# Moving the power of the degrees, and the turn of its result, from the head of the dilation into its turns

## The chip, the cores and the metric

The kernel runs on one core of one Trainium2 chip. The metric is the device time of one execution in microseconds (us). Before the change three timed executions took 2714.34, 2714.92 and 2715.22 us; their median, 2714.92 us, is the time before.

The engines are named as the profile names them: PE multiplies matrices (PEld loads its weights), DVE and ACT are the vector and the scalar engine, POOL is GpSimd, and SP issues most of the transfers. Each engine works through its own list of instructions in order and waits at an instruction until what it needs is there.

## The reference

Four layers of a graph network run one after the other on 16 batches of 1024 nodes with 128 features and one adjacency matrix per batch. Each layer adds its result to `x` and normalises the rows.

- Layer 0 is an attention over the neighbours with a gate.
- Layer 1 first dilates the adjacency matrix: row by row it removes some neighbours of a node, in the row and in the column, so that a row depends on the rows before it. Three graph convolutions with the dilated matrix follow.
- Layer 2 is a second gated attention with the original matrix.
- Layer 3 is a graph convolution with the original matrix, scaled on both sides by the inverse root of the degrees:

```python
def _gcn_norm(adj):
    A_hat = adj + jnp.eye(adj.shape[-1], dtype=adj.dtype)
    deg = A_hat.sum(axis=-1)
    dinv = jnp.where(deg > 0, jax.lax.rsqrt(deg), 0.0)
    return dinv[..., :, None] * A_hat * dinv[..., None, :]
```

`dinv` is what the changed lines compute. The degrees are summed in layer 0, while the matrices are read; nothing reads `dinv` before layer 3.

## The kernel before

**Stages.** In the profiled execution layer 0 runs to about 624 us, the dilation to about 1000 us, layer 1 to about 1670 us, and layers 2 and 3, interleaved batch by batch, to the end. A last piece computes a flag from several checks of the data, `nomem` among them.

**Degrees.** `deg` is a tile of 128 partitions by 128 columns (16 batches of 8 blocks). ACT fills it by the accumulator of the copy that turns the matrix into 8 bits (L931). `dinv` is another name for the same tile (L673), and `zeros` another name for `mx0` (L681), the row extrema of layer 0's attention. `mhalf` holds -0.5.

**The head of the dilation** (L1178 to L1188), in the order of the source: DVE compares `mx0` and reduces it to `nomem`; DVE writes `zeros` from `deg`, and the shifted degree into `deg`; POOL takes the power -1/2 in place (L1183); PE transposes the result into a PSUM tile `pt` that shares its two buffers with the tile `s` of the removals (L1185); DVE copies it into `dt` (L1187); SP stores `dt` into `dinv_d` in device memory (L1188). In layer 3 every batch reads `dinv_d` as a row (L1754) and `dinv` as columns (L1758).

**The dilation.** The rows are taken in 8 blocks of 128 and the batches in 2 groups of 8, which makes 16 steps. `prepare` counts a step's neighbours (products L1069 over four batches at a time; L1063, L1071 and L1072 on DVE). `fixed_point` finds the removals inside the block by iteration (L1092, L1097 and L1104 on DVE, products L1100). `removal` applies them for one batch: products L1144 and L1142 into `s`, ACT L1145, DVE L1148 and L1149, products L1152 to L1156, ACT L1157. A turn `i` interleaves the fixed point of step `i`, the removals of step `i - 1` and the preparation of the step after next. There are 16 turns.

**The end of layer 0** runs together with the first preparations and the first fixed point: `after` of the last batch, which ends in `normed`. Its row norm takes a power on POOL too (L745, 128 by 8 values, called from L797), between L742 on DVE before it and L799 on DVE behind it; then ACT scales the rows (L801, eight instructions) and POOL stores the result (L1019).

**What sets the order.** The source gives each instruction a place, but the framework's scheduler lists the instructions of each engine by its own model of when they are ready, with the place in the source as priority. An instruction can so stand on its engine far ahead of its place in the source. The kernel takes powers on POOL alone; POOL's list around this place is: power of the degrees, L745 of the last batch, L1019, and then nothing until the stores of the dilated matrices (L1159). SP's list is: the store L1188, layer 1's weights (L703, L693, L698), the loads of the dilated matrices (L1369).

Of the kernel before, what the change touches and what calls it, by code (L numbers as in the profile page):

```python
# [9 lines left out]
F32 = mybir.dt.float32  # L10
# [7 lines left out]
OP = mybir.AluOpType  # L18
AX = mybir.AxisListType
# [3 lines left out]
P = 128  # L23
# [616 lines left out]
def fast_kernel(ctx: ExitStack, tc: tile.TileContext, t: dict, out: bass.AP, flag: bass.AP):  # L640

    nc = tc.nc
    B, N, D = t["x"].shape
    NT = N // P
    H2 = N // 512
    BT = B * NT
# [4 lines left out]
    identf = consts.tile([P, P], F32, name="identf")  # L651
# [5 lines left out]
    mhalf = consts.tile([P, NT], F32, name="mhalf")  # L657
# [10 lines left out]
    dinv_d = dram.tile([BT, P], F32, name="dinv_d")  # L668
# [3 lines left out]
    deg = consts.tile([P, BT], F32, name="deg")  # L672
    dinv = deg  # L673
# [6 lines left out]
    mx0 = consts.tile([P, BT], F32, name="mx0")  # L680
    zeros = mx0  # L681
    nodeg = consts.tile([P, B], F32, name="nodeg")
    nc.vector.memset(nodeg, 1.0)
    nomem = consts.tile([P, 1], F32, name="nomem")
# [126 lines left out]
    def take_turns(streams):  # L811
        while streams:
            streams = [s for s in streams if next(s, streams) is not streams]
# [221 lines left out]
    with ExitStack() as ph:  # L1035
        sb = ph.enter_context(tc.tile_pool(name="dl_sb", bufs=2, side="right", reuse_waits="tile"))
# [3 lines left out]
        ps_s = ph.enter_context(tc.tile_pool(name="dl_ps", bufs=2, space=PSUM, side="right", reuse_waits="tile"))  # L1040
# [120 lines left out]
        def removals(now, then):  # L1161

            start = prepare(*then) if then else None
            for i in range(GB):
                removal(*now, i)
                yield
                if then and i % QB == QB - 1:
                    next(start)
                    yield
# [5 lines left out]
        ending.close()  # L1175
        ps_c = ph.enter_context(tc.tile_pool(name="dl_pc", bufs=2, space=PSUM, reuse_waits="tile"))

        nc.vector.tensor_scalar(mx0, mx0, 1.0e15, None, op0=OP.is_gt)  # L1178
        nc.vector.tensor_reduce(nomem, mx0, AX.X, OP.max)

        nc.vector.tensor_scalar(zeros, deg, -1.0, float(N), op0=OP.mult, op1=OP.add)
        nc.vector.tensor_scalar(deg, deg, 1.0, 1.0, op0=OP.add, op1=OP.max)
        nc.gpsimd.tensor_tensor(dinv, deg, mhalf[:, 0:1].to_broadcast([P, BT]), op=OP.pow)  # L1183
        pt = ps_s.tile([BT, P], F32, name="pt", tag="s")
        nc.tensor.transpose(pt, dinv, identf)  # L1185
        dt = sb.tile([BT, P], F32, name="dt", bufs=1)
        nc.vector.tensor_copy(dt, pt)  # L1187
        nc.sync.dma_start(dinv_d, dt)  # L1188

        for i in range(1, len(steps) + 1):  # L1190
            streams = [fixed_point(*steps[i])] if i < len(steps) else []
            streams.append(removals(steps[i - 1], steps[i - 1 + G2] if i - 1 + G2 < len(steps) else None))
            take_turns(streams)

    class Layers23:

# [640 lines left out]
def kernel(tc: tile.TileContext, t: dict, out: bass.AP):  # L1837
    nc = tc.nc
    with tc.tile_pool(name="flag", bufs=1) as pool:
        flag = pool.tile([1, 1], I32, name="flag")  # L1840
        fast_kernel(tc, t, out, flag)
        with tc.If(nc.values_load(flag[0:1, 0:1]) != 0):
            general_kernel(tc, t, out)
# [22 lines left out]
```

## Time and profile before

| What | Value |
|---|---|
| median of the timed executions | 2714.92 us |
| the profiled execution, its own time | 2712.03 us |
| span from its first to its last instruction | 2710.2 us |
| PE busy | 2540.1 us (94%) |
| DVE busy | 2085.2 us (77%) |
| ACT busy | 1977.6 us (73%) |
| POOL busy | 317.9 us (12%) |
| PE clock, mean of what was granted | 0.98 of full speed |
| POOL, power of the degrees (L1183), 128 by 128 values | 1 instruction, 20.74 us |
| POOL, power L745 of a norm, 128 by 8 values, typical | 1.66 us |
| SP, `dinv_d` stored | issued at 645.97 us |
| SP, `dinv_d` first read (L1754) | issued at 1673.3 us |

The profile is one execution with a record for each instruction. Shares of busy time are averages over stages that differ, so the prediction reads the stage around the change by itself: busy time by stage, who waited for whom, and the list of instructions in order of time. A wait that the profile shows is put down to the instruction that came last.

### The profile page before, as it was taken

How to read it: one execution, taken by the hardware profiler on the slowest of the kernel's cores; microseconds unless marked ns; L12 is line 12 of the kernel's file. 1: busy time of each engine (PE TensorE's matmuls, PEld its weight loads, DVE VectorE, ACT ScalarE, POOL GpSimd, SP SyncE). 2: the span in 40 equal slices, each digit the busy share in tenths (PEclk: the TensorE clock that was granted, in tenths of full speed). 3: DMA queues.
4: the chain of work that ended last, by engine and by line, in shares of the span. 5: the costliest groups of instructions: out<-in, count | busy, mean ns of one | idle time of the engine just before them, and what ended most of it. 6: DMA issues, size and time to landing. Idle time of an engine off the chain costs nothing.

```text
span 2710.2 us, 41446 instructions
## 1 busy us (share of the span) xinstructions
PE 2540.1 (94%) x14888; PEld 1677.4 (62%) x14888; DVE 2085.2 (77%) x5590; ACT 1977.6 (73%) x3188; POOL 317.9 (12%) x287
## 2 busy tenths in 40 slices
PE   8999999996889879999999998999999999999986
PEld 4445444443666647887788886466666666666655
DVE  6887778875799876776688876577877878787785
ACT  7888889874888866666655544777777777777773
POOL 0000000003000001111212133000110100001001
PEclk9999999996999989999999999999999999999998
DMA  5555555430000052233466664102212111111100
GB/s 190 161 174 171 172 163 179 156 117 23 2 2 2 2 207 75 95 106 128 139 227 212 250 231 181 39 24 70 78 70 85 71 63 63 63 63 63 47 24 25
DMA packets 120808, 285.34 MB, mean 105 GB/s; under 512 B 12305, under 2 KB 65425, under 8 KB 113425
## 3 DMA queue, kind: packets, MB, share of 16 engines
q1 hardware_dynamic: 101280, 203.33, 23.1%
q0 software_dynamic: 19312, 79.28, 7.6%
q8 instruction: 119, 1.95, 0.3%
q14 instruction: 97, 0.79, 0.1%
HBM read 202.72 MB, written 79.82 MB: 104 GB/s over the span
## 4 chain that ended last, share of the span: by engine, by line
PE 56%; DVE 16%; issue 7%; POOL 5%; ACT 4%; DMA 3%; POOLq 0%; ACTq 0%; DVEq 0%
PE ph L1618 8%; PE acc L1678 7%; PE acc L1306 6%; PE ph L766 5%; PE acc L973 5%; PE pmm L724 5%; PE ph L759 4%; PE ph L1432 3%; PE pmm L1690 3%; PE ph L1605 2%; DVE mid L1097 2%; DVE keep L1148 2%; POOL rn L745 2%; POOL ln_rstd L745 1%; ACT q L1145 1%
## 5 line engine op out<-in xcount | busy, mean ns | idle before, releaser
L745 POOL TENSOR_TENSOR ln_rstd<-ln_rstd,mhalf 128x8 f32<-128x8 f32 (+1 forms) x68 | 108.4, 1594 | 1332.0 <-DVE ln_rstd L742 861.4
L973 PE MATMUL acc<-em,hs 128*128 128x512 f32 x512 | 259.2, 607 | 2.5 <-DVE past L1075 1.3
L724 PE MATMUL pmm<-xT,G 128*128 128x512 f32 x512 | 259.8, 604 | 0.0
L1678 PE MATMUL acc<-ex,hs 128*128 128x512 f32 x512 | 248.9, 596 | 7.5 <-DVE hs L1705 4.5
L801 ACT ACTIVATE xn<-xn,ln_nb,ln_rstd 128x128 f32<-128x128 f32 x512 | 204.6, 481 | 55.3 <-DVE ln_nb L799 55.3
L1306 PE MATMUL acc<-a,hi 128*128 128x512 f32 x768 | 233.7, 398 | 12.0 <-DVE a L1293 9.0
L1306 PE MATMUL acc<-a,lo 128*128 128x512 f32 x768 | 230.1, 394 | 5.8 <-DVE lo L1273 5.8
L985 ACT ACTIVATE em<-em,mx 128x1024 f32<-128x1024 f32 x128 | 146.3, 1143 | 53.0 <-DVE mx L983 51.5
L983 DVE CUSTOM_DVE_ANT_0 em<-pmm,msk 128x1024 f32<-128x1024 f32 x128 | 156.1, 1220 | 31.9 <-PE pmm L724 30.7
L1698 ACT ACTIVATE ex<-em,mn 128x1024 f32<-128x1024 f32 x128 | 146.9, 1147 | 44.7 <-DVE mn L1695 44.0
L1690 PE MATMUL pmm<-G,hT 128*128 128x512 f32 (+3 forms) x416 | 175.3, 523 | 0.1
L1695 DVE CUSTOM_DVE_ANT_0 em<-pmm,msk 128x1024 f32<-128x1024 f32 x128 | 155.4, 1214 | 24.4 <-PE pmm L1692 22.3
L1306 PEld LDWEIGHTS acc<-a,hi 128*128 128x128 f32 x768 | 142.2, 189 | 43.5 <-DVE a L1293 11.5
L1306 PEld LDWEIGHTS acc<-a,lo 128*128 128x128 f32 x768 | 143.3, 189 | 41.1 <-DVE lo L1273 11.5
L1157 ACT ACTIVATE carry<-pc,negone 128x1024 fp8e4<-128x1024 f32 x128 | 141.3, 1115 | 27.6 <-PE pc L1156 24.8
L931 ACT ACTIVATE carry<-an 128x1024 fp8e4<-128x1024 f32 x128 | 134.4, 1050 | 31.3 <-DMA an<-in_adj 30.4
L980 ACT ACTIVATE msk<-carry,l0nbig 128x1024 bf16<-128x1024 fp8e4 x128 | 145.3, 1136 | 0.0
L1686 ACT ACTIVATE msk<-A,nbig 128x1024 bf16<-128x1024 fp8e4 x128 | 144.2, 1138 | 0.0
L1618 PE MATMUL ph<-A,hi 128*128 128x512 f32 x512 | 143.1, 420 | 0.8 <-DVE zn L1607 0.6
L1295 ACT CAST a<-A 128x1024 fp32r<-128x1024 fp8e4 x96 | 98.4, 1048 | 54.9 <-PE acc L1306 53.8
L1678 PEld LDWEIGHTS acc<-ex,hs 128*128 128x128 f32 x512 | 88.6, 190 | 76.8 <-issue 54.6
L1295 ACT CAST a<-carry 128x1024 fp32r<-128x1024 fp8e4 x96 | 99.1, 1047 | 47.8 <-PE acc L1306 47.5
(319 smaller groups left out, 6184.2 us busy)
## 6 DMA issues: line engine op xcount, KB each, us to landing
an<-in_adj SPq DMA_DIRECT2D x128, 512.0 KB, 3.7
adj_d<-carry POOLq DMA_DIRECT2D x16, 1024.0 KB, 4.2
A<-dil_d SPq DMA_DIRECT2D x16, 1024.0 KB, 5.3
rdeg<-rdeg_d SPq DMA_DIRECT2D x32, 512.0 KB, 4.1
A<-adj_d SPq DMA_DIRECT2D x16, 1024.0 KB, 5.0
ag_d<-ag POOLq DMA_DIRECT2D x24, 512.0 KB, 5.0
ag<-ag_d SPq DMA_DIRECT2D x24, 512.0 KB, 6.1
xn<-in_x SPq DMA_DIRECT2D x16, 512.0 KB, 4.3
```

The lines of the kernel that those rows point to most:

```text
L724: nc.tensor.matmul(p[:, h * 512:(h + 1) * 512], lhsT, rhs[:, h * 512:(h + 1) * 512], start=True, stop=True)
L745: nc.gpsimd.tensor_tensor(r, r, mhalf[:, :n], op=OP.pow)
L801: nc.scalar.activation(r[:, k.start + i, :], r[:, k.start + i, :], AF.Identity, scale=rstd[:, i:i + 1], bias=nb[:, i:i + 1])
L973: nc.tensor.matmul(s.acc[:, c], hs, em[:, c], start=(jt == 0), stop=(jt == NT - 1))
L983: nc.vector.tensor_tensor_reduce(em, e, msk, 1.0, 3.0e38, op0=OP.add, op1=OP.min, accum_out=mn)
L1295: nc.scalar.copy(a, A[:, 2 * i:2 * i + 2, c])
L1306: nc.tensor.matmul(acc, part[:, jt, :], pieces[h * NT // 2 + k][:, jt - 2 * k, :], start=(part is parts[0] and jt == 0), stop=(part is par ...
L1618: nc.tensor.matmul(p, part[:, jt, :], A[jt][:, c], start=(jt == 0 and i == 0), stop=(jt == NT - 1 and i == 1))
L1678: nc.tensor.matmul(s.acc[:, c], hs, ex[:, c], start=(jt == 0), stop=(jt == NT - 1))
L1690: nc.tensor.matmul(e[:, c], s.hT[:, js], s.G[:, c], start=True, stop=True)
L1695: nc.vector.tensor_tensor_reduce(row, e, msk, 1.0, 0.0, op0=OP.add, op1=OP.min, accum_out=mn)
L1698: nc.scalar.activation(ex, row, AF.Exp, scale=-1.0, bias=mn, accum_out=sm)
```

## The change

The eleven lines at the head of the dilation go into the loop over its turns. The DVE operations and the power are issued after the streams of turn 2, the transpose, its copy and the store after those of turn 6. The operations themselves are the same, and so are the tiles and the pools.

```diff
-        nc.vector.tensor_scalar(mx0, mx0, 1.0e15, None, op0=OP.is_gt)
-        nc.vector.tensor_reduce(nomem, mx0, AX.X, OP.max)
-
-        nc.vector.tensor_scalar(zeros, deg, -1.0, float(N), op0=OP.mult, op1=OP.add)
-        nc.vector.tensor_scalar(deg, deg, 1.0, 1.0, op0=OP.add, op1=OP.max)
-        nc.gpsimd.tensor_tensor(dinv, deg, mhalf[:, 0:1].to_broadcast([P, BT]), op=OP.pow)
-        pt = ps_s.tile([BT, P], F32, name="pt", tag="s")
-        nc.tensor.transpose(pt, dinv, identf)
-        dt = sb.tile([BT, P], F32, name="dt", bufs=1)
-        nc.vector.tensor_copy(dt, pt)
-        nc.sync.dma_start(dinv_d, dt)
-
         for i in range(1, len(steps) + 1):
             streams = [fixed_point(*steps[i])] if i < len(steps) else []
             streams.append(removals(steps[i - 1], steps[i - 1 + G2] if i - 1 + G2 < len(steps) else None))
             take_turns(streams)
+            if i == 2:
+                nc.vector.tensor_scalar(mx0, mx0, 1.0e15, None, op0=OP.is_gt)
+                nc.vector.tensor_reduce(nomem, mx0, AX.X, OP.max)
+
+                nc.vector.tensor_scalar(zeros, deg, -1.0, float(N), op0=OP.mult, op1=OP.add)
+                nc.vector.tensor_scalar(deg, deg, 1.0, 1.0, op0=OP.add, op1=OP.max)
+                nc.gpsimd.tensor_tensor(dinv, deg, mhalf[:, 0:1].to_broadcast([P, BT]), op=OP.pow)
+            elif i == 6:
+                pt = ps_s.tile([BT, P], F32, name="pt", tag="s")
+                nc.tensor.transpose(pt, dinv, identf)
+                dt = sb.tile([BT, P], F32, name="dt", bufs=1)
+                nc.vector.tensor_copy(dt, pt)
+                nc.sync.dma_start(dinv_d, dt)
```

## The prediction

> **What bounds the kernel now.** I began with the busy table: PE is busy 94% of 2710.2 us, so time can be won only where PE stands still. The forty slices show one such hole: PE at 6 of ten in the tenth slice, the only slice where POOL shows 3. The chain that ended last confirms it: POOL holds 5% of it, and in the stretch around the hole one POOL instruction is on it for 20.75 us. Busy time by stage, cut at the instruction's own ends (columns: stage, length, busy us and count for PE, PEld, DVE, ACT, POOL, then PE clock, DMA share, GB/s):
>
> ```profile
> 610.00:624.40 14.40, 12.60 (x59) 5.74 (x58) 8.50 (x35) 9.36 (x18) 2.65 (x3) 1.00 0.13 38
> 624.40:645.10 20.70, 1.61 (x34) 1.07 (x32) 1.17 (x5) 1.02 (x1) 20.68 (x1) 0.62 0.00 0
> 645.10:662.10 17.00, 13.53 (x125) 8.66 (x126) 13.65 (x58) 4.00 (x7) 1.80 (x1) 0.50 0.05 13
> 662.10:1000.00 337.90, 286.46 (x3710) 210.31 (x3709) 292.03 (x831) 274.70 (x366) 5.23 (x9) 0.95 0.08 29
> ```
>
> For 20.7 us everything but POOL is idle, and afterwards PE runs at half clock. Who waits for whom there (us in total, times, longest):
>
> ```profile
> ACT r L777 <- PE pq L775: 20.5, 1, 20.5
> ...
> PE pt L1185 <- POOL deg L1183: 19.1, 1, 19.1
> DVE dt L1187 <- PE pt L1185: 18.4, 1, 18.4
> POOL ln_rstd L745 <- DVE thr L1092: 15.2, 1, 15.2
> ...
> DVE ln_nb L799 <- POOL ln_rstd L745: 1.5, 1, 1.5
> ```
>
> The transpose L1185 waits for the power; the gate products L775 stand behind it on PE and ACT waits for them; on DVE the copy L1187 holds up the rest. The timeline (start, duration, instruction, idle before it):
>
> ```profile
> 624.35 20.74 POOL L1183 TENSOR_TENSOR deg<-deg,mhalf 128x128 f32<-128x128 f32 x1 [5.87 <-DVE deg L1182]
> ...
> 626.78 0.29 DVE L1063 TENSOR_TENSOR uY<-carry,upper 128x128 int32<-128x128 int32 x1
> ...
> 645.14 0.48 PE L1185 MATMUL pt<-identf,deg 128*128 128x128 f32 x1 [19.13 <-POOL deg L1183]
> ...
> 645.54 1.08 PE L775 MATMUL pq<-hpT,l0gw 128*32 128x256 f32 x8
> 645.65 0.29 DVE L1187 COPY dt<-pt 128x128 f32<-128x128 f32 x1 [18.43 <-PE pt L1185]
> ...
> 660.24 1.80 POOL L745 TENSOR_TENSOR ln_rstd<-ln_rstd,mhalf 128x8 f32<-128x8 f32 x1 [15.16 <-DVE thr L1092]
> ...
> 662.08 0.17 DVE L799 SCALAR_TENSOR_TENSOR ln_nb<-ln_mv,ln_rstd 128x8 f32<-128x8 f32 x1 [1.53 <-POOL ln_rstd L745]
> ```
>
> The next POOL instruction, the power of the last batch's norm (L745), comes 15.16 us after the long one ended. Those 15 us, not the 20, will turn out to be the prize.
>
> [...]Where DVE was first, POOL lost time:
>
> ```profile
> 1772.11 1.21 DVE L1752 TENSOR_TENSOR A<-A,identb 128x1024 fp8e4<-128x1024 fp8e4 x1
> 1772.37 2.45 POOL L745 TENSOR_TENSOR ln_rstd<-ln_rstd,mhalf 128x8 f32<-128x8 f32 x1 [22.67 <-ACT msk L1686]
> ```
>
> That is 2.45 us against the usual 1.64 to 1.66. But L1063 above reads two SBUF tiles, starts 2.43 us into the long power and takes 0.29 us, as it does outside it (0.28 at 649.59). The power does not shut DVE out for its length; the measurement decides. [...]Here PE stops at 626.02 and the clock mean of 0.79 for 629 to 630 puts the drop at about 629.6, that is 3.6 us.
>
> **The change, part by part.** Source order and built order differ: the framework lists each engine's instructions by readiness in its own model. Comparing the two built programs, the four DVE operations and the power do not move at all. On DVE they still stand between an L1063 and an L1071 of the opening preparation, and on POOL the power is still directly ahead of the last L745. What moves is the tail: the transpose goes on PE to just ahead of the last L1100 group but one of turn 6, the copy on DVE to behind L1117 a little later, the store on SP from ahead of the layer 1 weight loads to behind them, still ahead of the first dil_d load. Around the new place a few L1142, L1144, L1148, L1063 and L1071 swap neighbours; the rest is unchanged apart from semaphore names.
>
> *Removed at the head.* PE's 19.1 us wait, DVE's 18.4 us, and 0.48 + 0.29 us of work. L775 can follow the end of hpT (625.14 + 1.02 = 626.16) at about 626.25 instead of 645.54: 19.3 us earlier. DVE's L1089 follows L1087 at 627.2 instead of 645.86: 18.7 us earlier. From there to L742 the chain is nearly all DVE work, so L742 moves from 659.94 to about 641.
>
> *What is late next.* POOL is in order and still busy until 624.35 + 20.74 = 645.09. So L745 starts there, 4 us after its input (L742's, though the waits name L1092) is ready, and takes 1.65: it ends at about 646.8 instead of 662.04. L799 on DVE and the eight L801 on ACT wait for it, and behind them in order everything of DVE and ACT, then PE at L1100. From L799 on the two kernels have the same order, so the head gains 662.04 − 646.8 = 15.2 us, not 19.3. The chain of waits should show a DVE wait on L745 of 5.5 to 6 us in place of 1.5.
>
> *The power under traffic.* Before, it ran beside an idle DVE; now DVE works beside it. The DVE operations with two SBUF inputs between L1089 and L742, with L1148 counted in, are L1097 (2 × 1.23), L1013 and L1016 (1.22 each), L1113 (2 × 0.29), L1063 (0.28), L1148 (0.74), L1149 (0.42) and ten small ones (about 0.12 each in a row): 8.1 us. If each stopped POOL's reading[...], the power would last 8 us longer; that is the upper bound. The lower is 0. A power of 8 columns takes 1.64 and one of 128 takes 20.74, so 0.16 us a column; a 1.65 us power that starts 0.02 us ahead of a 0.69 us cast (1121.52) loses nothing, [...]1.22 us is the work of 7.7 columns. I take 0.7 us.
>
> *The clock.* PE was at half clock from 645.1 to 662.1 and mostly until 673.9. The part to 662 is hidden under POOL now. In the chain after it PE holds 5.6 us between 668.1 and 673.7, worth 2.8 us at full clock. But PE stops again: its work ends at about 644.3 and mid L1097 lets it go on at about 648.3. That 4 us pause is beside the 3.6 measured, so the clock may drop anew. Bounds 0 and 2.8, taken 0.5.
>
> *Added in turn 6* (780 to 790 us). PE gets the transpose in the place of an L1144 that moves back: nothing. The second half's L1142 group used to run at 784.29 and now waits for the copy dt, until about 786.6; ACT reads it at 788.12, so it is covered. DVE is packed there from 783.7 to 789.6 and gets 0.29 us. I take a loss of 0.3, bounds 0 and 1.5 (if the swapped order misses a turn of ACT, 0.69, and of DVE, 0.75). The store: SP is idle from 674.7 to 1000.1, the first reader (L1754) issues at 1673.3: hidden.
>
> *Sum*: 15.2 − 0.7 + 0.5 − 0.3 = 14.7 us. Against the profiled execution, span 2710.2 and time 2712.03: 2695.5 and 2697.3. The timed runs have a median of 2714.92, 2.9 above the profiled one; I subtract from that: **2700.2 us**, 0.54% faster. About 0.2%, 5.4 us, is what a measurement of this kernel tells from no change.
>
> **Rivals.** (1) *Full clock as well* (0.15): the pause stays under 3.6 us; 15.2 + 2.8 − 0.5 = 17.5, 2697.4.[...] (2) *The power is starved* (0.18): 3 to 8 us longer, 2702.5 to 2708; for it the 2.45 us case, against it the 1121 one and L1063. (3) *The power locks DVE out* (0.07)[...]: the first mid L1097 waits for 645.1 instead of starting at 646.26; gain 1 to 3 us, about 2713, no change. L1063 speaks against it. (4) *Slower* (0.05): PE stays on half clock after the new pause. In the stage to 1000 us PE is busy 85% of the time at 0.95 clock; at half clock the work takes about 1.6 times as long, so each cold microsecond loses about 0.4. It decides when the cold spell lasts 37 us longer than now (14.7 / 0.4); at 50 us more, 2720. Against it: the present cold spell ended after about 6 us of dense matmuls. That the transpose is not moved is excluded by the built order; that the power is not moved is true, and is in the forecast.
>
> **How the numbers follow.** The main case has 0.55 (2698 to 2702). Faster: 0.55 + 0.15 + 0.18 = 0.88; same 0.07; slower 0.05. The range 2696.5 to 2708 holds the main case and rivals 1 and 2 nearly whole, leaving out some 0.14.
>
> **What would show it.** Right: the power at about 624 with 20.7 to 21.5 us, PE busy beside it, L745 starting as it ends, a wait of 5 to 6 us at L799, the transpose near 770 with no long wait. Wrong: a power over 23 us, an L1097 of many us or a gap ahead of it, PE clock 0.5 through the first turn, or a wait at the store or at L1142 in turn 6.

## The result

The changed kernel takes 2695.56 us (median of six executions, 2691.40 to 2698.95); the kernel before, beside it, 2714.63 us (2712.28 to 2715.22). The ratio is 0.993 with a 95% interval of 0.9917 to 0.9943: faster by 15 to 23 us, 19.1 us by the medians. The forecast was 2700.2 us with a range of 2696.5 to 2708: the direction and the mechanism at the head held, the gain was put too low, and the time lies 0.9 us below the range.

The profiled execution of the changed kernel has a span of 2693.2 us (before: 2710.2), 17.0 us less. Busy time by stage in the changed kernel, cut at the power's ends and at L799 (columns as before: stage, length, busy us and count for PE, PEld, DVE, ACT and POOL, PE clock, DMA share, GB/s):

```profile
613.14:624.10 10.96, 9.15 (x51) 4.24 (x50) 5.76 (x19) 7.26 (x15) 0.93 (x1) 1.00 0.16 48
624.10:644.80 20.70, 15.08 (x170) 9.96 (x168) 14.56 (x61) 5.03 (x8) 20.70 (x1) 0.67 0.00 1
644.80:646.50 1.70, 0.00 (x0) 0.00 (x0) 0.01 (x1) 0.00 (x0) 1.66 (x2) 1.00 0.00 0
646.49:978.72 332.23, 280.49 (x3687) 206.66 (x3687) 289.57 (x817) 272.95 (x363) 5.24 (x9) 0.97 0.07 27
```

The 20.7 us in which PE was busy for 1.6 us and DVE for 1.2 us are now 15.1 and 14.6 us of work beside a power that is as long as before. In the 1.7 us behind it only POOL works: that is L745. The timeline and the waits of the changed kernel (its line 1188 is the power, formerly L1183):

```profile
624.10 20.74 POOL L1188 TENSOR_TENSOR deg<-deg,mhalf 128x128 f32<-128x128 f32 x1 [5.87 <-DVE deg L1187]
...
625.98 0.64 PE L775 MATMUL pq<-hpT,l0gw 128*32 128x256 f32 x8 [0.21 <-ACT hpT L1001]
...
627.42 1.23 DVE L1097 TENSOR_TENSOR mid<-sk,thr 128x1024 fp8e4<-128x1024 f16 x1
...
640.07 0.16 DVE L742 TENSOR_SCALAR ln_rstd<-ln_mv 128x8 f32<-128x8 f32 x1
...
644.82 1.63 POOL L745 TENSOR_TENSOR ln_rstd<-ln_rstd,mhalf 128x8 f32<-128x8 f32 x1
646.49 0.17 DVE L799 SCALAR_TENSOR_TENSOR ln_nb<-ln_mv,ln_rstd 128x8 f32<-128x8 f32 x1 [5.80 <-POOL ln_rstd L745]
```

```profile
PE pd L1100 <- DVE mid L1097: 6.2, 2, 4.7
...
DVE ln_nb L799 <- POOL ln_rstd L745: 5.8, 1, 5.8
...
ACT xn L801 <- DVE ln_nb L799: 4.7, 1, 4.7
```

The transpose's wait of 19.1 us is gone from the list. In its place stands one of 5.8 us: L745's input is ready once L742 is done, at 640.2 us, but L745 starts only as the power ends, with no gap, and DVE, ACT and PE wait for it one behind the other.

### The profile page after: what moved, and what is told of

Its sections match the earlier page's. It is cut to its first block, busy times and chain, and to the rows that moved or that the text cites. A ratio compares the mean times of both kernels' runs of the same rounds, so it can differ in the third digit from the quotient of the medians.

```text
span 2693.2 us, 41450 instructions
## 1 busy us (share of the span) xinstructions
PE 2539.0 (94%) x14888; PEld 1677.9 (62%) x14888; DVE 2085.4 (77%) x5590; ACT 1977.5 (73%) x3188; POOL 317.7 (12%) x287
## 4 chain that ended last, share of the span: by engine, by line
PE 58%; DVE 16%; issue 6%; ACT 4%; POOL 4%; DMA 2%; POOLq 0%; ACTq 0%; DVEq 0%
PE ph L1619 8%; PE acc L1679 7%; PE acc L1307 7%; PE ph L766 5%; PE acc L973 5%; PE pmm L724 5%; PE ph L759 4%; PE ph L1433 4%; PE pmm L1691 3%; PE ph L1606 2%; DVE mid L1097 2%; DVE keep L1148 2%; POOL ln_rstd L745 1%; POOL rn L745 1%; ACT q L1145 1%
## 5 line engine op out<-in xcount | busy, mean ns | idle before, releaser
L745 POOL TENSOR_TENSOR ln_rstd<-ln_rstd,mhalf 128x8 f32<-128x8 f32 (+1 forms) x68 | 108.3, 1593 | 1318.7 <-DVE ln_rstd L742 864.2
```

The lines of the kernel that those rows point to most:

```text
L745: nc.gpsimd.tensor_tensor(r, r, mhalf[:, :n], op=OP.pow)
```

## The experiments

One number carries most of them: the time from the last but one L799 of layer 0 to its last. Both ends are the same instruction, one batch apart, and the head of the dilation lies between. The table has it for all kernels, with the time from that last L799 to the third L1107 (L1107 on DVE comes once behind each of the 16 fixed points; in this stretch full clock comes back, 8.8 to 11.9 us behind L799), that to the sixteenth and last L1107 (the rest of the dilation), and the timed ratio.

| Kernel | L799 to L799, us | to third L1107, us | to last L1107, us | Ratio to before, 95% interval |
|---|---|---|---|---|
| before | 48.70 | 31.27 | 334.28 | |
| e1, before again | 48.70 | 31.16 | 334.00 | 0.9995 (0.9987 to 1.0003) |
| changed | 33.35 | 30.13 | 332.23 | 0.9930 (0.9917 to 0.9943) |
| e2, changed again | 33.35 | 31.09 | 333.87 | 0.9935 (0.9921 to 0.9948) |
| e3, tail only | 33.36 | 31.15 | 333.95 | 0.9939 (0.9926 to 0.9953) |
| e4, late power | 28.93 | 30.16 | 332.81 | 0.9921 (0.9908 to 0.9935) |
| e5, power twice | 54.14 | 30.30 | 332.08 | 1.0022 (1.0013 to 1.0031) |
| e6, half early | 29.06 | 30.18 | 332.65 | 0.9926 (0.9910 to 0.9943) |
| e7, all in turn 2 | 33.34 | 30.20 | 335.80 | 0.9954 (0.9938 to 0.9971) |

**e1, the kernel before once more.** No edit.

> The kernel before, run as if it were a change, to learn how far executions of one program differ and where. Theory A (the 15.3 us gained at L799 and about 1 us behind it are all that the change does, the rest of the measured 19.1 us is scatter): ratio 1.000, the profile within 3 us of 2710.2, and the differences against the first profile lie in stages that the change does not touch. Theory B (the change gains 2 to 3 us more in later stages): ratio 1.000 too, but the later stages of this profile repeat the first one within 0.5 us.

Its span was 2712.7 us, 2.5 more than the first profile's. The head repeats to the hundredth (48.70), the dilation within 0.3 us. What differs is layer 1: from the first power of its first convolution (`rn`) to that of its first batch norm (`brstd`) 341.99 us against 339.87, and to the second 196.48 against 194.86. No line of the change runs there. Timed executions of the kernel before went from 2706.3 to 2717.7 us over the two chips of these experiments. The later stages do not repeat within 0.5 us, so Theory B loses the sign it named for this run.

**e2, the changed kernel once more.** No edit.

> The changed kernel once more. Theory A: 16 to 17 us faster, ratio 0.9939; L799 again 15.3 us earlier counted from the start of the power, and later stages that come out differently than in the first profile. Theory B: 19 us or more, ratio 0.9930 or less, with the same extra gain in the same later stage as in the first profile.

Median 2695.78 us against 2712.95, 17.2 us less; the ratio's 0.65% is 17.6 us, between the two theories. The profile decides: 33.35 us at the head as in the first one, but layer 1's first part took 341.52 us here against 339.26 there. Within one program, that is as much as the "extra" that was to be explained. The span was 2698.1 us, 4.9 more than the first profile of the same program.

The head does not follow PE or DVE here. PE's clock was halved earlier in this execution (from about 624.1 us, in the first profile from 628.0), so L742 came 17.2 us behind the start of the power (624.41 us) instead of 16.0, and DVE waited 4.59 us at L799 instead of 5.80; L745 (645.13 us) and L799 still stand where the end of the power puts them:

```profile
641.59 0.17 DVE L742 TENSOR_SCALAR ln_rstd<-ln_mv 128x8 f32<-128x8 f32 x1
...
646.80 0.17 DVE L799 SCALAR_TENSOR_TENSOR ln_nb<-ln_mv,ln_rstd 128x8 f32<-128x8 f32 x1 [4.59 <-POOL ln_rstd L745]
```

What differs in layer 1's first part is the PE clock too. In the five profiles that keep full clock there (before, changed, e5, e6, e7) it takes 338.8 to 340.9 us; in the four with one spell of 3.4 us at half clock (e1 to e4) 341.5 to 342.7. The spell of e1 (PE clock third from the end); at the same place in the kernel before, 288 us behind the first `rn`, the clock is 1.00:

```profile
1329.50:1332.90 3.40, 3.40 (x10) 2.61 (x9) 2.98 (x6) 1.04 (x1) 0.35 (x1) 0.51 0.42 140
```

Half of such a spell, 1.7 us, is the most that it can cost by itself (an estimate from its 3.40 us at a clock of 0.51), so it can account for most of the 2.3 us between the means of the two groups, not for all. The second part of layer 1 sorts the same way (194.2 to 195.0 us without a spell, 195.6 to 196.7 with one or two), the third does not. Why an execution has a spell or not is not shown.

**e3, only the tail moved.** The five operations on `mx0`, `zeros` and `deg`, the power among them, stay at the head; only the transpose, the copy and the store go to turn 6. Against the changed kernel, cut:

```diff
+        nc.vector.tensor_scalar(mx0, mx0, 1.0e15, None, op0=OP.is_gt)
...
+        nc.gpsimd.tensor_tensor(dinv, deg, mhalf[:, 0:1].to_broadcast([P, BT]), op=OP.pow)
+
         for i in range(1, len(steps) + 1):
...
-            if i == 2:
...
-            elif i == 6:
+            if i == 6:
```

> Only the transpose, its copy and the store go to turn 6; the DVE operations and the power stay in the source at the head. If the move of the power does nothing, as the built order says, this is the changed kernel: ratio as e2 within 0.1%, the power at about 624 us, L745 straight behind it. Rival (the power's place matters): slower than e2 by 1 us or more.

Ratio 0.9939, head 33.36 us, power at 625.06 us and L745 straight behind it: the changed kernel, within 0.1%. The first part of the edit, the move of the power and of the four operations before it to turn 2, does nothing. The built order of the engines is the same instruction for instruction, so this is also a third profile of one program.

**e4, the power really late.** Its exponent comes from a tile that DVE writes in turn 2 out of a value of that turn; the order of PE, DVE and ACT is otherwise that of the changed kernel:

```diff
+                mh = tiny.tile([P, 1], F32, name="mh", bufs=1)
+                nc.vector.tensor_scalar(mh, steps[2][0].wid[:, 0:1], 0.0, -0.5, op0=OP.mult, op1=OP.add)
-                nc.gpsimd.tensor_tensor(dinv, deg, mhalf[:, 0:1].to_broadcast([P, BT]), op=OP.pow)
+                nc.gpsimd.tensor_tensor(dinv, deg, mh[:, 0:1].to_broadcast([P, BT]), op=OP.pow)
```

> The exponent of the power is read from a tile that DVE writes in turn 2, so that the power can't start before; on POOL it now stands behind the last L745. Theory A (POOL's queue ends the head: L745 waits 4.7 us for the power in the changed kernel): L745 starts at about 640.2, L799 is another 4 to 4.7 us earlier, PE has no pause of 4.7 us there and keeps full clock, which may give 0 to 2 us more; 20.7 to 23 us of power in turns 2 to 4 cost nothing: 2688 to 2692 us, ratio 0.990 to 0.992. Rival C (the power slows the dense DVE work beside it[...]): DVE operations with two inputs are longer beside the power, and the gain at L799 is given back, ratio 0.993 or more. Rival D (the wait at L799 was not what the head ended on): ratio as e2.

POOL and L799 at the head, and the power beside the turns with the DVE operations there, in e4's timeline:

```profile
642.27 1.81 POOL L745 TENSOR_TENSOR ln_rstd<-ln_rstd,mhalf 128x8 f32<-128x8 f32 x1 [21.99 <-DVE thr L1092]
...
644.12 0.17 DVE L799 SCALAR_TENSOR_TENSOR ln_nb<-ln_mv,ln_rstd 128x8 f32<-128x8 f32 x1 [1.55 <-POOL ln_rstd L745]
...
677.82 20.74 POOL L1191 TENSOR_TENSOR deg<-deg,mh 128x128 f32<-128x128 f32 x1 [29.10 <-DVE mh L1190]
...
687.57 1.22 DVE L1097 TENSOR_TENSOR mid<-sk,thr 128x1024 fp8e4<-128x1024 f16 x1
```

The wait at L799 is back to 1.55 us and the head takes 28.93 us, 4.42 less than in the changed kernel: the 4 us that the forecast had L745 wait. Beside the dense turns the power takes 20.74 us and a two-input L1097 1.22: neither slows the other, and Rival C falls. The rest of the dilation is not longer than in the other kernels. One part of Theory A missed: PE had no pause of 4.7 us behind the head (its longest wait between L799 and the drop was 1.77 us), but its clock was halved all the same from 651.1 to 654.5 us, and the stretch to the third L1107 is no shorter than in the first profile of the changed kernel. Median 2691.88 us against 2712.95, ratio 0.9921, a hair above the upper end of what Theory A gave.

**e5, the power twice.** The same power is taken once more, into `dt`, ahead of the real one:

```diff
+                dt = sb.tile([BT, P], F32, name="dt", bufs=1)
+                nc.gpsimd.tensor_tensor(dt, deg, mhalf[:, 0:1].to_broadcast([P, BT]), op=OP.pow)
                 nc.gpsimd.tensor_tensor(dinv, deg, mhalf[:, 0:1].to_broadcast([P, BT]), op=OP.pow)
...
-                dt = sb.tile([BT, P], F32, name="dt", bufs=1)
```

> The changed kernel with the same power of 128 by 128 values taken once more into the tile dt ahead of the real one, so that POOL is busy 20.7 us longer before the last L745. Theory A (POOL's queue ends the head): L745 starts about 41.5 us after the first power's start, the stretch between the last two L799 is 33.35 + 20.7 = 54.1 us and the time 20 to 21 us more than the changed kernel, a little above the kernel before: ratio 1.000 to 1.003. Rival (the head ends on DVE, PE or ACT, POOL is beside it): the time of the changed kernel, ratio 0.994.

POOL in e5, and the wait it causes:

```profile
623.43 20.74 POOL L1189 TENSOR_TENSOR dt<-deg,mhalf 128x128 f32<-128x128 f32 x1 [5.88 <-DVE deg L1187]
644.25 20.71 POOL L1190 TENSOR_TENSOR deg<-deg,mhalf 128x128 f32<-128x128 f32 x1
664.93 1.63 POOL L745 TENSOR_TENSOR ln_rstd<-ln_rstd,mhalf 128x8 f32<-128x8 f32 x1
```

```profile
DVE ln_nb L799 <- POOL ln_rstd L745: 26.7, 1, 26.7
```

20.8 us more on POOL make the head 20.79 us longer (54.14 against 33.35), and the kernel 0.22% slower than before. POOL, 12% busy over the span, is the engine that ends the head of the changed kernel.

**e6, half of the power early.** As e4, but the first 64 columns keep `mhalf`:

```diff
-                nc.gpsimd.tensor_tensor(dinv, deg, mh[:, 0:1].to_broadcast([P, BT]), op=OP.pow)
+                hb = BT // 2
+                nc.gpsimd.tensor_tensor(dinv[:, :hb], deg[:, :hb], mhalf[:, 0:1].to_broadcast([P, hb]), op=OP.pow)
+                nc.gpsimd.tensor_tensor(dinv[:, hb:], deg[:, hb:], mh[:, 0:1].to_broadcast([P, hb]), op=OP.pow)
```

> The power is cut in two: 64 columns at the head, the other 64 held back as in e4. The first takes about 10.6 us and is over at about 635, ahead of L742 at about 640. Theory A: the wait at L745 is gone as in e4, the stretch between the last two L799 is 28.9 us, ratio 0.992. If the loss were in proportion to the power's length: 31 us.

```profile
624.37 10.54 POOL L1192 TENSOR_TENSOR deg<-deg,mhalf 128x64 f32<-128x64 f32 x1 [5.87 <-DVE deg L1188]
640.62 1.81 POOL L745 TENSOR_TENSOR ln_rstd<-ln_rstd,mhalf 128x8 f32<-128x8 f32 x1 [5.72 <-DVE thr L1092]
```

10.54 us at the head cost next to nothing: POOL stands idle for 5.72 us ahead of L745, and the head takes 29.06 us, 0.13 more than in e4, not the 31 of a proportional loss. With e4, e5 and the changed kernel this is a bend: up to the moment at which L745's input is ready the power is free, beyond it each microsecond counts in full. Median 2690.25 us against 2711.29: e4 and e6 both come out ahead of the changed kernel's ratio, though the timed intervals overlap; the heads, 28.9 and 29.1 against 33.35 us, do not.

**e7, everything behind turn 2.** The transpose, the copy and the store follow the power in the same branch:

```diff
-            elif i == 6:
```

> All eleven lines behind turn 2, so that the transpose, the copy and the store come some 95 us earlier than in the changed kernel, but still behind the end of the power. Theory A: the place of the tail does not matter once it stands behind the power: 33.35 us between the last two L799 and the ratio of the changed kernel within 0.1%. Rival (turn 2 is denser for PE or DVE, and the shared buffer costs a turn there): 0.5 to 2 us slower up to the dilation's end.

The head is the changed kernel's (33.34 us), but the ratio is 0.9954, outside what Theory A allowed, though its interval still overlaps those of the changed kernel. The loss is in the turns: from the third to the eighth L1107 117.96 us against 114.40 in e2, 3.6 us more, of which 0.7 comes back later. That is the rival's direction: counted from L799, the last L1107 comes 1.9 us later than in e2 and 3.6 later than in the first profile of the changed kernel, where the rival named 0.5 to 2. The clock is not the reason: 3.4 of the 3.6 us are there by the seventh L1107, at 774.5 us, and from 657.6 us up to then PE had full clock. In the built program a good part of PE's and DVE's order from turn 3 to turn 6 comes out differently from the changed kernel's, not only next to the transpose. That the different order costs the 3.6 us is inferred from where they appear; which of its waits does it was not followed.

## Why the prediction was wrong, and what of it was right

**Right: what bounds the head, and what is late next.** L775 starts at 625.98 us (about 626.25 was said, for a power that started 0.25 us later), L742 at 640.07 (about 641), L745 as the power ends, and the wait at L799 is 5.8 us (5.5 to 6), though only 4.6 and 4.9 in e2 and e3, where the clock brought L742 later (0.74 in the mean over the head in both, 0.80 in the first profile). The head gains 48.70 - 33.35 = 15.35 us; the step said 15.2, and not the 19.3 by which PE's and DVE's work moved up. e5, e4 and e6 show the cause by lengthening, removing and halving it.

**Right: the power was not moved.** e3 shows it.

**Right: no lock for the power's length.** Rival 3 had DVE stand still until the power ends. The traces show none of that: with the power first, neither of the two L1097 beside it was held up (1.23 and 1.22 us), nor any of the three in e4 (1.22 to 1.23); the 76 of the kernel take 1.21 to 1.23 us before and after the change.

**Wrong: the power under traffic.** The term of 0.7 us is 0.00: 20.74 us beside idle DVE, beside the head's work, and beside the dense turns of e4. The rival with a starved power, 0.18 of the chance and most of the range's upper part, rested on the same fear. The 2.45 us case was real, but there the power starts while a DVE instruction with two SBUF inputs is already running (0.26 us into L1752's 1.21 us). No long power of these runs starts at such a moment, so what it would lose then is not shown. The case at 1121.52 says little either way: the cast there, which took 0.73 us, reads one tile.

**Between its bounds: the clock.** 0.5 us was taken between bounds of 0 and 2.8, and the runs show two cases. From L799 to the third L1107 the changed program took 30.13 us once and 31.09 and 31.15 in e2 and e3; the kernel before 31.27 and 31.16. So the gain is about 1.1 or 0.1 us, and that 0.5 lies near their mean is luck. In the four microseconds that differ most (windows of the changed kernel, then of e2, eight us behind L799; PE clock third from the end):

```profile
654.49:658.49 4.00, 3.76 (x48) 3.05 (x47) 2.49 (x5) 3.55 (x5) 0.00 (x0) 0.90 0.24 58
```

```profile
654.80:658.80 4.00, 4.00 (x42) 3.37 (x41) 1.29 (x3) 2.85 (x4) 0.00 (x0) 0.57 0.28 61
```

What sorts all nine profiles is the moment at which full clock comes back. Where it does so 8.8 to 10.4 us behind L799 (changed, e4, e5, e6, e7), the stretch takes 30.1 to 30.3 us; where it does so 11.4 to 11.9 us behind (before, e1, e2, e3), 31.1 to 31.3. Counted from L799, the changed program had it back at 8.8 us in its first profile and at 11.4 us in e2, 2.6 us apart for the same instructions.

Rival 1, full clock as well, did not come, and its condition was not the right one: it asked for a pause under 3.6 us, an estimate from the one drop in the profile of before. (Its sum of 17.5 us takes off 0.5 where the forecast's own 0.7 and 0.3 make 1.0; that gives 17.0.) In e2 the pause of PE ahead of L1100 was 2.8 us, and the clock was halved again at 648.0 us all the same. Nor did rival 4: that second spell lasted 6.8 us in the changed kernel and 10.2 in e2 and e3.

**Wrong in sign, small: turn 6.** A loss of 0.3 us was put down; from the sixth to the eighth L1107 the changed program takes 49.70 to 49.71 us and the kernel before 49.77 to 49.80, a gain of 0.1. The transpose and the copy run as forecast (engine, operation, count, duration in ns, start):

```profile
L1191 PE MATMUL pt<-identf,deg x1: 303/303/303, 765.3 to 765.3; 128*128 128x128 f32 x1
```

PE stood idle for 1.07 us ahead of it, in a place where it used to wait 1.02 us for ACT's L1145; the turn is not longer for it. The profile names no cause; an L1145 had ended just before, at 765.2 us, which fits the buffer that `pt` shares with `s`.

**The sum.** With the measured terms it is 15.35 + 0.00 + 0.1 to 1.1 + 0.1, that is 15.6 to 16.6 us, where 14.7 stood: one to two us too little, most of it the 0.7 of the traffic and the 0.4 of turn 6.

**The step that failed: how the range followed.** It was made of the cases alone: 7.8 us upwards for the starved power and 3.7 us downwards. How far executions of one program lie apart is no term of it, although the forecast itself put at 5.4 us what a measurement of this kernel tells from no change, and the time of before was taken as known. The executions show that scatter: those of one program lie 7 to 9 us apart on one chip, and 8 to 11 us over all the chips used (2706.3 to 2717.7 before, 2691.4 to 2699.8 changed). A median of six is still uncertain by several us, as the interval of the first ratio, 7 us wide, says. Of the 4.6 us between the forecast and 2695.56, 0.3 is the base (2714.63 instead of 2714.92) and 0.9 to 1.9 are the terms above; the other 2.5 to 3.5 us are in no stage that repeats. A sum of 16 us gives 2698.9, and 4 us to either side, about half of that scatter, would have held 2695.56.

**What stays open.** The timed ratios of this program are 0.9930, 0.9935 and 0.9939, 16.5 to 19.1 us, the profiles' spans differ by 15.2 us in the mean (2710.2 and 2712.7 before; 2693.2, 2698.1 and 2697.4 changed), and the stages add up to about 16. All intervals hold 16 us; that the change gains 1 to 3 us somewhere else is not excluded, but no stage shows it twice. The time of an execution goes with the PE clock granted in it: of e3's five, the one at 0.984 took 2692.23 us, the one at 0.982 2695.35, and the three at 0.980 2698.65 to 2699.54. In e5's eleven the tie is loose. That spells of half clock make most of the scatter is likely from this and from layer 1, but not shown.

## What to carry to other kernels

When a wait is taken off an engine, follow the engine that caused it: here POOL's own queue, not the transpose, set when the next POOL result came, and the gain was the gap behind the long instruction, not the length of the wait. Where a scheduler lists the instructions by readiness, as here, moving a line may move nothing that is ready early (e3); a data dependency does move it (e4), and moving a line elsewhere can reorder whole turns (e7). Ask how far executions of one program scatter before making a range narrower than that.

## What the runs showed of the hardware

- A 128 by 128 power on POOL takes 20.74 us (20.71 straight behind another), 64 columns 10.54 us and most of those of 8 columns (97 of 108 in the kernel before, 99 of 108 in the changed one) 1.63 to 1.67 us: about 0.16 us a column and 0.4 us for the instruction (an estimate from these times). The 20.74 us were the same beside an idle DVE (busy for 1.2 of 20.7 us, before) and beside a busy one (14.6 of 20.7 us, changed); one power of 8 columns that starts 0.26 us into a DVE instruction with two SBUF inputs took 2.45 us (L745 at 1772.37 us in the kernel before).
- In the traces of the kernel before and of the changed one, each spell of half clock of PE, but the one in which the execution ends, lasts 3.41, 6.83, 10.24, 13.65 or 34.13 us: 1, 2, 3, 4 or 10 times 3.41. In two executions of one program full clock came back at different instructions, 8.8 us behind L799 in the first profile of the changed kernel and 11.4 us in e2; from L799 to the third L1107 they took 30.13 and 31.09 us.
- PE fell to half clock while it worked. In the changed kernel it did at 628.0 us, with no pause over 1.3 us in the ten us before; the same program in e2 was at half clock from about 624.1 and came back at about 627.5. Windows of the changed kernel, one us each:

```profile
627.00:628.00 1.00, 1.00 (x33) 1.00 (x34) 0.92 (x3) 0.06 (x1) 1.00 (x1) 0.99 0.00 0
628.00:629.00 1.00, 1.00 (x8) 1.00 (x7) 1.00 (x2) 0.00 (x0) 1.00 (x1) 0.50 0.07 16
```

By the profile's account PE is busy for the whole of both, and its clock is halved in the second. No long pause stands ahead of this drop; what brought it is not shown.
